# A third output tile in two PSUM banks, and a depthwise convolution's taps placed behind the softmax

## The chip, the cores and the metric

The kernel runs on one core of a Trainium2 chip. The metric is the device time of one execution in microseconds (us); the median of three executions before the change is 3747.22 us (3746.66 to 3749.31). Engines are named as in the profile: PE is TensorE (PEld its weight loads), DVE is VectorE, ACT is ScalarE, POOL is GpSimd, SP issues most of the transfers. All data are fp32. A difference of less than 0.2% is taken as no difference.

## The reference

The input x has 8 images of 384 channels and 64 x 64 pixels. Two layers follow each other, each added to its own input:

```python
x = x + attention(gn(x))     # layer norm, qkv, windowed attention, projection
x = x + ffn(gn(x))           # 1x1 convolution, 8x8 transform, depthwise 3x3, gate, 1x1 convolution
```

`gn` is a group normalisation over an image. The attention works in windows of 8 x 8 pixels, with 4 heads of 48 channels in plain windows (branch 0) and 4 in windows shifted by 4 pixels (branch 1): softmax(q k^T + position bias + mask) v, then a projection. The second layer is

```python
t = conv1x1(x, w_in); t = irfft2(rfft2(t in 8x8 patches) * filter)
t = depthwise3x3(t, w_dw)              # 9 taps for each channel
g = gelu(t[:192]) * t[192:]
y = conv1x1(g, w_out)                  # 192 -> 384 channels
```

The last line is the one whose third output tile the change splits.

## The kernel before

An image is cut into 8 strips of 8 rows (512 pixels). 384 channels are three tiles of 128 partitions. Every step of a strip is a small Python function, and a plan gives each step a place in time, counted in units: a unit is one attention branch of one strip, so an image has 16 units. The steps of all images are sorted by place and issued in that order (L803 to L819). The second layer of an image runs in the units of the next ones: while the attention of image b + 1 passes through its units, the strips of image b go through `normal_x1`, `mix`, `transform`, `back`, `conv`, `gate` and `finish`, one strip for two units. `finish` of a strip stands at place 0.10 of an even unit, 8 units or more after the start of the next image. So every even unit from unit 8 of image 1 on has one finish (images and units are counted from 0): 52 of them beside attention, and 12 in the tail after the last image's attention.

On PE the program's order is kept (`matmul`, L61). On DVE, ACT and POOL a scheduler of the framework orders instructions inside their dependencies, and moves some forward where it expects the engine to be idle; `behind` (L289) gives it an extra ordering on one engine. `conv` (L658) does one tap of the depthwise convolution for one channel tile m, the first tap on ACT (L667) and eight on DVE (L673). Taps 1 to 5 have places soon after the strip's `back` (for m = 0 in the same even unit, 0.68 to 0.92; for m = 2 and 1 in the odd one), taps 6 to 8 in the next even unit. Tap 6 is ordered behind the softmax's subtraction (`zs["soft"]`, L463).

The order of an even unit on PE is: `back` (pz), `apply` of the unit before (pA), `scores` (pS), `finish` (pw), the first `qk_tile` (pq), `put` of the unit before (po), then `mix` (pt) and `qk_tile` in turn, `turn` (pT), `v_tile` (pvv) and the layer norm's sums (ln). On DVE `normalise` (L503, L504) reads pA, `weights` (L456 to L463) reads pS and makes the softmax's exponents, L706 in `finish` adds pw to the residual, L535 to L537 move po.

[...] Tag "gemm" (`psum`) has four buffers of one bank: pq, pvv, ln, pt, pf, pz, pr and pw. Tag "att" (`psum2`) has two buffers of two banks: pS, pT, pA, po, and for the last image pc. A pool's buffers go round in order of allocation, and an allocation waits until the readers of the buffer's last tile are done.

`finish` makes its three output tiles from g0 (128 channels) and g1 (64 channels, held twice, in partitions 0 to 63 and 64 to 127). The g1 part is done by matmuls of 64 rows and 64 columns, a quarter of the array each, half naming the columns and r the rows:

```python
for m, half, r in ((0, 0, 0), (1, 1, 1), (0, 1, 0), (1, 0, 1), (2, 0, 0), (2, 1, 1)):
```

Then g0's part of each tile is accumulated by a full matmul, and DVE adds the tile to the residual.

A last piece is a plan of empty instructions. PE's runs of small tiles (pA, pS and their neighbours) need many instructions in little time. `FETCHES` has for every step how many instructions PE fetches (four for a matmul, two for a transpose), `WAITS` estimates those that only wait, and at the places of `small_tiles` the loop at L805 adds so many NoOps to the dense steps before (`qk_tile`, `project`) that the run begins at a given place (`RUN_AT`) of 256; if 100 or more would be needed, none are added.

Of the kernel before, what the change touches and what calls it, by code (L numbers as in the profile page):

```python
# [9 lines left out]
ALU = mybir.AluOpType  # L10
AX = mybir.AxisListType

P = 128
KC = 3
# [3 lines left out]
ST = WS * SW  # L18
# [10 lines left out]
N_CONST = C_SWAP + 128  # L29
WAITS = 5.325, -22  # L30
FETCHES = {"qk_tile": 12, "v_tile": 24, "project": 12, "scores": 128, "apply": 128, "turn": 16, "put": 16,
           "ln_sums": 64, "mix": 12, "transform": 32, "back": 192, "finish": 36, "input_mean": 4,
           "input_std": 4, "second_mean": 4, "second_std": 4, "filter_weights": 4, "out_bias": 36,
           "qk_weights": 48, "v_weights": 60}
RUN_AT = 208, 138
# [3 lines left out]
def block_kernel(ctx: ExitStack, tc: tile.TileContext, out, x, consts, fsel, wqk, wv, bqk, bv,  # L39
                 wp, bp, lng, lnb, rpb1, rpb2, w_in, w_dw, w_out, filt):  # L40
    nc = tc.nc
    B = x.shape[0]
# [7 lines left out]
    def psum(name):  # L50
        return ps.tile([P, ST], F32, tag="gemm", name=name)

    def psum2(name):

        return ps.tile([P, 2, ST], F32, tag="att", bufs=2, name=name)
# [5 lines left out]
    def matmul(*args, **kw):  # L61
        tc.keep_in_program_order(nc.tensor.matmul(*args, **kw))  # L62
        fetched["count"] += 4

        n = min(fetched["empty"], fetched["share"])
        for _ in range(n):
            tc.keep_in_program_order(nc.tensor.nop(hint="empty"))
        fetched["empty"] -= n
        fetched["count"] += n
# [5 lines left out]
    def strip(tag, bufs, name):  # L75
        return sb.tile([P, KC, ST], F32, tag=tag, bufs=bufs, name=name)

    def row512(tag, bufs, name):
        return sb.tile([P, ST], F32, tag=tag, bufs=bufs, name=name)
# [4 lines left out]
    def rows_of(img, s):  # L84

        return img[:, s * WS:(s + 1) * WS, :].rearrange("(p k) h w -> p k (h w)", k=KC)

    first_x = []
    for s in range(NS):
        tag, bufs = ("x", 5) if s < 5 else (("xn", 1), ("ow", 1), ("y2", 1))[s - 5]  # L90
        t = strip(tag, bufs, f"x_first{s}")
# [28 lines left out]
    wo_sb = cp.tile([P, 2, C], F32, name="wo_sb")  # L120
# [44 lines left out]
    for br, tab in ((0, rpb1), (1, rpb2)):  # L165
        raw = sb.tile([P, 2, 64], F32, tag="t2", bufs=3, name=f"rpb_raw{br}")
        raw_bias.append(raw)
        for h in range(4):
            half = slice(h % 2 * 64, h % 2 * 64 + 64)
# [110 lines left out]
    xs, ys, y2s, qks, vs, os_, ots, x1s, zs = ({} for _ in range(9))  # L280
# [8 lines left out]
    def behind(i, other, kind, reason):  # L289
        tc.add_manual_dep(i.ins, other.ins.name, mybir.DependencyInfo(kind, mybir.DependencyReason.DATA),  # L290
                          reason=reason)
# [366 lines left out]
    def conv(b, s, m, tap):  # L658

        z = zs[b, s, m]  # L660
        n = on_pe[s].get(m, 0) if b == B - 1 else 0
        if tap < max(n, 1):
            return
        if tap == max(n, 1):
            zz = row512("zz", 5, f"zz_{b}_{s}_{m}")
            if n == 0:
                nc.scalar.activation(zz.rearrange("p (r c) -> p r c", c=SW), z[:, 1:9, 1:SW + 1], AF.Copy,  # L667
                                     scale=dw_sb[:, m, 4:5])
                zs[b, s, "zz", m] = zz
            zs[b, s, "acc", m] = zz  # L670
        acc, old = zs[b, s, "acc", m], zs[b, s, "zz", m]
        dy, dx = TAPS[tap] // 3, TAPS[tap] % 3
        i = nc.vector.scalar_tensor_tensor(acc.rearrange("p (r c) -> p r c", c=SW),  # L673
                                           z[:, dy:dy + 8, dx:dx + SW], dw_sb[:, m, TAPS[tap]:TAPS[tap] + 1],
                                           old.rearrange("p (r c) -> p r c", c=SW), ALU.mult, ALU.add)

        if b < B - 1 and m and tap == 1:
            tc.keep_in_program_order(i)
        if b < B - 1 and tap == 6:
            behind(i, zs["soft"], mybir.DependencyClass.NoSync, "softmax first")  # L680
        zs[b, s, "zz", m] = acc

# [10 lines left out]
    def finish(b, s):  # L693


        g0, g1 = zs[b, s, "g"]
        t = xs[b, s, "finish"]
        pw = [psum(f"pw_{b}_{s}_{m}") for m in range(KC)]

        for m, half, r in ((0, 0, 0), (1, 1, 1), (0, 1, 0), (1, 0, 1), (2, 0, 0), (2, 1, 1)):  # L700
            rows, cols = slice(r * 64, (r + 1) * 64), slice(half * 64, (half + 1) * 64)
            matmul(pw[m][cols], wo_sb[rows, 1, m * P + half * 64:m * P + half * 64 + 64], g1[rows],
                   start=True, stop=False)
        for m in range(KC):
            matmul(pw[m], wo_sb[:, 0, m * P:(m + 1) * P], g0, start=False, stop=True)
            zs["added"] = nc.vector.tensor_tensor(t[:, m, :], pw[m], t[:, m, :], ALU.add)  # L706
        nc.sync.dma_start(out=rows_of(out[b], s), in_=t)


# [3 lines left out]
    for b in range(B):  # L713
# [62 lines left out]
        for s in range(NS):  # L776
            u = first + 2 + 2 * s
            at(u - 0.84, load, b, s, "mix")
            at(u + 0.02, normal_x1, b, s)
            for i in range(4):  # L780
                at(u + (0.28, 0.45, 0.60, 0.78)[i], mix, b, s, i)
            for j in range(2):
                at(u + (0.995, 1.02)[j], transform, b, s, j)
            if b < B - 1:
                at(u + 1.985, small_tiles, u + 2)
            at(u + 1.99, back, b, s)

            for n, m in enumerate((0, 2, 1)):
                for tap in range(1, 6):
                    at(u + (2.62, 3.15, 3.5)[n] + 0.06 * tap, conv, b, s, m, tap)  # L790
                for tap in range(6, 9):
                    at(u + 4.2 + 0.25 * (n * 3 + tap - 6) / 9, conv, b, s, m, tap)
            if b == B - 1:
                at(u + 2.3, conv_taps, b, s)
            at(u + 5.16, load, b, s, "finish")
            at(u + 4.5, gate, b, s)
            at(u + 6.10, finish, b, s)
# [7 lines left out]
    for i, (piece, args) in enumerate(order):  # L805
# [5 lines left out]
        elif piece is small_tiles:  # L811
            n = (RUN_AT[args[0] % 2] - count - round(WAITS[0] * args[0] + WAITS[1])) % 256
# [115 lines left out]
```

## Time and profile before

| what | before |
|---|---|
| median of three executions | 3747.22 us |
| profiled execution, its time | 3747.89 us |
| its span | 3745.9 us |
| PE busy | 3638.7 us, 97% of the span |
| PE weight loads | 2315.4 us, 62% |
| DVE busy | 2838.6 us, 76% |
| ACT busy | 2378.3 us, 63% |
| POOL busy | 439.2 us, 12% |
| HBM traffic | 99 GB/s over the span |
| granted TensorE clock | 0.996 |

The span is what the trace covers; the execution's own time has 2 us more around it. The busy time of PE is modelled at the ends of matmuls, so that 97% says that PE always has something in hand, not that every part of its array works. In the groups, the line L62 is the helper that records all matmuls, so matmuls are told apart by their tiles: pw is finish's.

### The profile page before, as it was taken

Reading aid. Unit: us, or ns where it says so; the run is one execution under the profiler, and the core shown is the slowest. Engines: PE = TensorE matmul, PEld = TensorE weight load, DVE = VectorE, ACT = ScalarE, POOL = GpSimd, SP = SyncE. Lnnn points to the kernel's source line nnn. Section 1 sums busy time; section 2 is a strip of 40 time slices with the busy share of each in tenths; the row PEclk is TensorE's granted clock in tenths of the full one; section 3 lists DMA queues with packets and bytes.
Section 4 is the critical chain, followed back from the end, with each engine's and each line's share of the span. In section 5 each row is a group of like instructions: output and inputs, shape, how many; then the busy total and the mean of one; then the engine's idle time right before and its main releaser. Section 6 shows DMA issues by size and latency. Waiting matters only on the chain.

```text
span 3745.9 us, 92754 instructions
## 1 busy us (share of the span) xinstructions
PE 3638.7 (97%) x38144; PEld 2315.4 (62%) x38144; DVE 2838.6 (76%) x4601; ACT 2378.3 (63%) x3946; POOL 439.2 (12%) x776
## 2 busy tenths in 40 slices
PE   4999999999999999999999999999999999999898
PEld 3666666666666666666666666666666666666554
DVE  4554578777887687777887778877788777777898
ACT  1766676666676576665766766666676666676442
POOL 5111011111101011101101011111111111110000
PEclk9999999999999999999999999999999999999999
DMA  4222222323322233323332322323233222222422
GB/s 121 86 83 74 91 100 100 107 90 108 118 103 83 88 133 108 116 80 116 109 113 84 117 95 100 133 80 109 99 113 109 99 88 83 100 80 82 151 102 76
DMA packets 144506, 377.32 MB, mean 101 GB/s; under 512 B 12308, under 2 KB 12900, under 8 KB 144100
## 3 DMA queue, kind: packets, MB, share of 16 engines
q1 hardware_dynamic: 139952, 370.60, 28.3%
q8 instruction: 318, 5.21, 0.6%
q0 software_dynamic: 2048, 0.15, 0.1%
q10 hardware_dynamic: 2100, 0.63, 0.1%
q14 instruction: 88, 0.72, 0.1%
HBM read 270.54 MB, written 100.79 MB: 99 GB/s over the span
## 4 chain that ended last, share of the span: by engine, by line
PE 84%; DVE 6%; ACT 4%; DMA 3%; issue 2%; POOL 0%; SPq 0%; ACTq 0%; DVEq 0%; POOLq 0%
PE pq L62 23%; PE pr L62 13%; PE pt L62 12%; PE pvv L62 12%; PE pw L62 6%; PE pS L62 3%; PE pA L62 3%; PE pz L62 3%; DVE zz L673 3%; PE pT L72 3%; PE po L72 2%; PE pf L62 2%; PE ln L62 2%; PE pc L62 1%; DMA rpb_raw<-in_rpb_dram 1%
## 5 line engine op out<-in xcount | busy, mean ns | idle before, releaser
L673 DVE SCALAR_TENSOR_TENSOR zz<-z,dw_sb,zz 128x512 f32<-128x512 f32 x1490 | 1105.9, 760 | 195.4 <-ACT zz L667 172.7
L62 PE MATMUL pq<-y,wqk_sb 128*128 128x512 f32 x2160 | 990.2, 596 | 0.0
L62 PEld LDWEIGHTS pq<-y,wqk_sb 128*128 128x128 f32 x2160 | 402.7, 190 | 456.2 <-issue 424.2
L62 PE MATMUL pt<-wi_sb,xn 128*128 128x384 f32 x1536 | 535.2, 487 | 8.1 <-DVE x_finish L706 8.1
L62 PE MATMUL pr<-oT,wp_sb 128*128 128x512 f32 x1152 | 523.1, 592 | 1.0 <-DVE oT L537 1.0
L62 PE MATMUL pvv<-wv_sb,y 128*128 128x192 f32 x2880 | 496.5, 326 | 2.5 <-ACT kcd L394 2.5
L62 PEld LDWEIGHTS pvv<-wv_sb,y 128*128 128x128 f32 x2880 | 471.6, 190 | 40.1 <-issue 21.3
L394 ACT ACTIVATE qab<-pq,bq_sb,cst 96x512 f32<-96x512 f32 (+1 forms) x256 | 198.0, 773 | 402.9 <-PE pq L62 386.0
L62 PEld LDWEIGHTS pt<-wi_sb,xn 128*128 128x128 f32 x1536 | 286.0, 190 | 213.9 <-issue 49.0
L394 ACT ACTIVATE kcd<-pq,vec 32x512 f32<-32x512 f32 x512 | 348.9, 681 | 9.0
L62 PEld LDWEIGHTS pr<-oT,wp_sb 128*128 128x128 f32 x1152 | 211.1, 190 | 224.4 <-issue 209.7
L376 POOL COPY y<-y 128x384 f32<-128x384 f32 x112 | 100.2, 894 | 1583.1 <-PE pvv L62 1089.3
L349 DVE TENSOR_TENSOR lr<-m 128x128 f32<-128x128 f32 x64 | 19.7, 308 | 301.9 <-ACT m L347 301.8
L335 POOL TENSOR_TENSOR sq<-sq 128x512 f32<-128x512 f32 x128 | 167.8, 1311 | 637.2 <-ACT sq L333 632.2
L667 ACT ACTIVATE zz<-z,dw_sb 128x512 f32<-128x512 f32 x183 | 133.8, 733 | 166.1 <-PE pw L62 160.5
L394 ACT ACTIVATE qcd<-pq,bq_sb,cst 96x512 f32<-96x512 f32 (+1 forms) x256 | 197.3, 771 | 43.8 <-PE pq L62 40.4
L546 DVE SCALAR_TENSOR_TENSOR x_add<-pr,vec,x_add 128x512 f32<-128x512 f32 x192 | 143.4, 747 | 103.3 <-PE pr L62 101.5
L584 ACT COPY t<-pt 128x384 f32<-128x384 f32 x256 | 125.0, 488 | 141.6 <-PE pt L62 138.7
L428 ACT COPY v<-pvv 128x384 f32<-128x384 f32 x256 | 121.8, 481 | 129.7 <-PE pvv L62 129.3
L62 PE MATMUL pw<-zz,wo_sb 128*128 128x512 f32 x384 | 181.9, 610 | 0.0
L394 ACT ACTIVATE kab<-pq,vec 96x512 f32<-96x512 f32 (+1 forms) x256 | 174.4, 681 | 9.1 <-PE pq L62 7.4
L469 ACT ACTIVATE e<-e 128x1024 f32<-128x1024 f32 x128 | 135.3, 1057 | 68.2 <-DVE e L463 66.8
(139 smaller groups left out, 5272.6 us busy)
## 6 DMA issues: line engine op xcount, KB each, us to landing
x_add<-in_x_dram SPq DMA_DIRECT2D x64, 768.0 KB
x1d<-x_add SPq DMA_DIRECT2D x64, 768.0 KB
x_mix<-x1d SPq DMA_DIRECT2D x64, 768.0 KB
x_finish<-x1d SPq DMA_DIRECT2D x64, 768.0 KB
out_dram<-x_finish SPq DMA_DIRECT2D x64, 768.0 KB
x_norm<-in_x_dram SPq DMA_DIRECT2D x61, 768.0 KB
x_stats<-in_x_dram SPq DMA_DIRECT2D x56, 768.0 KB
rs<-line SPq DMA_DIRECT2D x62, 256.0 KB
```

The source lines that it names most:

```text
L62: tc.keep_in_program_order(nc.tensor.matmul(*args, **kw))
L72: tc.keep_in_program_order(nc.tensor.transpose(*args, **kw))
L335: nc.gpsimd.tensor_tensor(sq[:, 0, :], sq[:, 0, :], sq[:, k, :], ALU.add)
L349: nc.vector.tensor_tensor(rc, m[:, 0:P], m[:, 0:P], ALU.mult)
L376: nc.gpsimd.tensor_copy(dst[:, :, :, :, 0:4], src[:, :, :, :, 4:8])
L394: return nc.scalar.activation(dst[to:to + n], pq[of:of + n], AF.Identity, bias=bias[of:of + n], scale=scale)
L428: nc.scalar.copy(v[:, 2 * g:2 * g + 2, :, 0:HD], pvv[:, 0:384].rearrange("p (g h d) -> p g h d", g=2, h=4))
L469: nc.scalar.activation(e, e, AF.Exp)
L546: nc.vector.scalar_tensor_tensor(t[:, m, :], pr, bp_sb[:, m:m + 1], t[:, m, :], ALU.add, ALU.add)
L584: nc.scalar.copy(t1, pt[:, 0:C])
L667: nc.scalar.activation(zz.rearrange("p (r c) -> p r c", c=SW), z[:, 1:9, 1:SW + 1], AF.Copy, scale=dw_sb[:, m, 4:5])
L673: i = nc.vector.scalar_tensor_tensor(acc.rearrange("p (r c) -> p r c", c=SW), z[:, dy:dy + 8, dx:dx + SW], dw_sb[:, m, TAPS[tap]:TAPS[tap] ...
```

## The change

`finish` keeps two tiles in the gemm pool and takes its third from attention's pool: the first 256 pixels of tile 2 go to one bank of that buffer, the last 256 to the other. The g1 part of tile 2 becomes four quarter matmuls of 256 columns instead of two of 512, the g0 part two full matmuls of 256 columns instead of one of 512. The three adds follow after all matmuls in program order; the third reads both banks in one instruction. The count of finish in `FETCHES` becomes 48. In `conv`, tap 1 of tile 0 is ordered behind the softmax as tap 6 already was; taps 2 to 5 of tile 0 follow it, since each adds to the result of the one before. Where this holds (all images but the last), it is the softmax of branch 0 of the even unit in which the taps are placed.

```diff
@@ -29,7 +29,7 @@
 FETCHES = {"qk_tile": 12, "v_tile": 24, "project": 12, "scores": 128, "apply": 128, "turn": 16, "put": 16,
-           "ln_sums": 64, "mix": 12, "transform": 32, "back": 192, "finish": 36, "input_mean": 4,
+           "ln_sums": 64, "mix": 12, "transform": 32, "back": 192, "finish": 48, "input_mean": 4,
@@ -676,7 +676,7 @@
         if b < B - 1 and m and tap == 1:
             tc.keep_in_program_order(i)
-        if b < B - 1 and tap == 6:
+        if b < B - 1 and (tap == 6 or m == 0 and tap == 1):
             behind(i, zs["soft"], mybir.DependencyClass.NoSync, "softmax first")
         zs[b, s, "zz", m] = acc
@@ -695,15 +695,23 @@
         g0, g1 = zs[b, s, "g"]
         t = xs[b, s, "finish"]
-        pw = [psum(f"pw_{b}_{s}_{m}") for m in range(KC)]
-
-        for m, half, r in ((0, 0, 0), (1, 1, 1), (0, 1, 0), (1, 0, 1), (2, 0, 0), (2, 1, 1)):
+
+        pw = [psum(f"pw_{b}_{s}_{m}") for m in range(2)]
+        pw2 = psum2(f"pw2_{b}_{s}")
+        full, lo, hi = slice(0, ST), slice(0, 256), slice(256, ST)
+        pw = [(pw[0], 0, full), (pw[1], 1, full), (pw2[:, 0, lo], 2, lo), (pw2[:, 1, lo], 2, hi)]
+
+        for i, half, r in ((0, 0, 0), (1, 1, 1), (0, 1, 0), (1, 0, 1), (2, 0, 0), (3, 1, 1), (2, 1, 0), (3, 0, 1)):
+            p, m, tok = pw[i]
             rows, cols = slice(r * 64, (r + 1) * 64), slice(half * 64, (half + 1) * 64)
-            matmul(pw[m][cols], wo_sb[rows, 1, m * P + half * 64:m * P + half * 64 + 64], g1[rows],
+            matmul(p[cols], wo_sb[rows, 1, m * P + half * 64:m * P + half * 64 + 64], g1[rows, tok],
                    start=True, stop=False)
-        for m in range(KC):
-            matmul(pw[m], wo_sb[:, 0, m * P:(m + 1) * P], g0, start=False, stop=True)
-            zs["added"] = nc.vector.tensor_tensor(t[:, m, :], pw[m], t[:, m, :], ALU.add)
+        for p, m, tok in pw:
+            matmul(p, wo_sb[:, 0, m * P:(m + 1) * P], g0[:, tok], start=False, stop=True)
+        for m in range(2):
+            nc.vector.tensor_tensor(t[:, m, :], pw[m][0], t[:, m, :], ALU.add)
+        by_half = t[:, 2, :].rearrange("p (o n) -> p o n", o=2)
+        zs["added"] = nc.vector.tensor_tensor(by_half, pw2[:, :, lo], by_half, ALU.add)
         nc.sync.dma_start(out=rows_of(out[b], s), in_=t)
```

## The prediction

> **What bounds the kernel now.** I read the page's busy times and its chain first:
>
> ```profile
> span 3745.9 us, 92754 instructions
> PE 3638.7 (97%) x38144; PEld 2315.4 (62%) x38144; DVE 2838.6 (76%) x4601; ACT 2378.3 (63%) x3946; POOL 439.2 (12%) x776
> ...
> PE 84%; DVE 6%; ACT 4%; DMA 3%; issue 2%; POOL 0%; SPq 0%; ACTq 0%; DVEq 0%; POOLq 0%
> ```
>
> PE is busy for 97% and carries 84% of the chain; the rest is mostly the first 60 us and the last 220. Next the groups, kept apart by shape, and PE's own waits:
>
> ```profile
> L673 DVE SCALAR_TENSOR_TENSOR zz<-z,dw_sb,zz 128x512 f32<-128x512 f32 x1490 | 1105.9, 760 | 195.4 <-ACT zz L667 172.7 <-ACT z L632 10.9
> ...
> L62 PE MATMUL pw<-zz,wo_sb 128*128 128x512 f32 x384 | 181.9, 610 | 0.0
> ...
> L62 PE MATMUL pw<-g,wo_sb 64*64 64x512 f32 x768 | 131.6, 611 | 5.1 <-DVE g L688 5.1
> ```
>
> ```profile
> PE pz L62 <- DVE t L601: 8.9, 15, 3.0
> PE pt L62 <- DVE x_finish L706: 8.1, 6, 1.4
> ...
> PE pvv L62 <- ACT kcd L394: 2.5, 6, 0.6
> ```
>
> In the middle of the run PE waits for almost nothing: what shortens PE's own work there shortens the kernel, one for one. The one regular wait is pt's for the residual add, 6 times 1.35 us. Then one `finish` in the timeline (unit 10 of image 4), rows of PE, its weight loads and DVE:
>
> ```profile
> 1995.68 1.54 DVE L673 SCALAR_TENSOR_TENSOR zz<-z,dw_sb,zz 128x512 f32<-128x512 f32 x2 [3.60 <-ACT zz L667]
> ...
> 1996.11 0.25 PEld L62 LDWEIGHTS pw<-g,wo_sb 64*64 64x64 f32 x8
> ...
> 1996.16 1.93 PE L62 MATMUL pw<-g,wo_sb 64*64 64x512 f32 x11
> 1996.65 0.14 PEld L62 LDWEIGHTS pw<-g,wo_sb 64*64 64x64 f32 x2 [0.29 <-issue]
> 1997.08 0.14 PEld L62 LDWEIGHTS pw<-g,wo_sb 64*64 64x64 f32 x2 [0.29 <-issue]
> 1997.13 0.25 DVE L503 RECIPROCAL rc<-pA 128x16 f32<-128x16 f32 x1
> 1997.30 0.70 DVE L673 SCALAR_TENSOR_TENSOR zz<-z,dw_sb,zz 128x512 f32<-128x512 f32 x1
> 1997.92 0.95 DVE L504 TENSOR_TENSOR o<-pA,rc 128x768 f32<-128x768 f32 x1
> ...
> 1998.03 2.84 PE L62 MATMUL pw<-zz,wo_sb 128*128 128x512 f32 x6
> ```
>
> Each fp32 matmul shows as two loads and two matmul instructions. The first four quarter matmuls (eight loads in a bunch) run four at a time: two rounds of 0.43 us. The third tile's two run as a pair, two more rounds of 0.43 (loads at 1996.65 and 1997.08), with half of the array idle. And two taps stand on DVE before L503, so pA is released only at 1998.87, 2.7 us after pw begins.
>
> [...] Here a 512-column fp32 instruction takes 429 ns and a 192-column one (pvv, 12 in 1.95 us) 163[...]: so my estimate for 256 columns is 216 ns. [...]
>
> **The change, part by part.**
>
> *Third tile, part of g1.* It removes two rounds of 429 ns and adds two of 216: minus 0.43 us. All four quarters at short length are shown by pf (16 instructions of 192 columns in 0.66 us, 0.165 per four). Loads of 64x64 take 0.03 us each in a bunch, under the running round.
>
> *Third tile, part of g0.* Two instructions of 429 become four of 216: plus 0.006. Weights of 128x128 keep up at 192 columns (pvv), so they do at 256. The last add still covers 512 elements, 0.68 us. Net, minus 0.42 us a finish.
>
> *Buffers.* Attention's two double banks rotate pA, pS, [pw2], po. So pw2 waits until normalise (L503, L504) has read pA, and po for the bias adds L456 instead of L504. Behind pw2 on PE stand the rest of finish, the pq of the unit and everything after it. Its first load is due 0.49 us after pw begins, its matmul at 0.92. pA ends 0.72 before pw; in the built order L503 now follows at once, since the taps come after L463. L503 + L504 take 1.25: L504 ends at about +0.57 and the matmul could start at about +0.68 (0.1 for the handover, an estimate from L706 to pt). Hidden, 0.24 us to spare. DVE is idle by then: in these units its last other work ends 2.6 us or more before pw. Without that cover the stall is as long as DVE is late. po comes over 2.5 us after pw ends, the L456 are done at about +2: nothing.
>
> *Finish takes two gemm buffers instead of three.* The ring of four moves on by one: pt's first tile now takes a pz buffer that ACT has read, and no longer pw's first.
>
> *Taps.* In the even units five taps (3.7 us of DVE) move behind the softmax. L463 ends at about +7.3 (pw end 4.1, last add 0.7, L460 1.2, L463 1.2) where it was +9.4 or later, so the work after it ends at most 1.6 us later. DVE's idle time before L349 in the units concerned is 2.9 us at least; less 0.4 for the shorter unit, 0.9 is left. The next late item would be the layer norm's row, not needed for a unit more. These taps issue no DMA; SP's order stays, POOL's border memsets and ACT's zz move by a few places in units with idle time there.
>
> *Instruction blocks.* The built PE program has 768 fetches more and 636 NoOps fewer. The runs of small tiles begin at places 204 to 211 of 256, where they began at 198 to 211. Before, odd units lie 0.15 us on average over their shortest 25.73 at either end of this: nothing, plus or minus 2 us in all.
>
> Now the places that differ: units 2 and 4 of images 2 to 7, and the tail. Rows of DVE and PE there, image 3:
>
> ```profile
> 1329.47 1.46 DVE L328 TENSOR_SCALAR y<-x_norm,gs_a 128x512 f32<-128x512 f32 x3 [0.57 <-DMA x_norm<-in_x_dram]
> 1330.85 0.25 DVE L503 RECIPROCAL rc<-pA 128x16 f32<-128x16 f32 x1
> 1331.14 0.96 DVE L504 TENSOR_TENSOR o<-pA,rc 128x768 f32<-128x768 f32 x1
> ```
>
> ```profile
> 1350.67 2.22 PE L62 MATMUL pvv<-wv_sb,y 128*128 128x192 f32 x12 [0.36 <-ACT kcd L394]
> ...
> 1390.20 2.20 PE L62 MATMUL pt<-wi_sb,xn 128*128 128x384 f32 x6 [1.35 <-DVE x_finish L706]
> ```
>
> *Unit 2.* pw begins at 1330.29, L504 ends at 1332.10 (+1.80) behind work that keeps its place, so pw2 stalls. In the six images L504 ends at +1.66, 1.80, 2.04, 1.89, 1.04, 0.62: over +0.75 (here the first two rounds are done at 0.86) that is 4.7 us. PE's pvv wait later in the unit (0.3 to 0.6, five times, 2.2) hangs on a chain that begins with L463, which comes about 3 us earlier: gone.
>
> *Unit 4.* L504 ends at +1.35 (last image 0.55). There pw's other buffers were late too (zz at +2.18); with the stall zz begins at about +1.97: minus 0.21 five times, 0.42 once. The pt wait of 1.35 goes: 8.1.
>
> *Tail, 12 finishes.* The first is bound by DVE (no idle from 3479 to 3516), the next two or three too (PE waits 2.97 and 1.24 for L601): nothing. Then six periods of 21.14 us in which PE is first and DVE only 0.2 us behind: 0.2 each, 1.2. The very last, 0.4.
>
> Sum: 40 ordinary finishes x 0.414 = 16.6; unit 2: 6 x 0.414 - 4.7 + 2.2 = 0.0; unit 4: 1.5 + 8.1 = 9.6; tail 1.6. Together 27.8 us. The profiled execution took 3747.9 (span 3745.9), so 3720.1; it is 0.7 over the median of 3747.2, so 3719.4.
>
> **Rivals.**
>
> *A, the waits at the image's start only change their owner.* pt or a later tile waits for something else, pvv's wait stays: 27.8 - 8.1 - 2.2 = 17.5, so 3730. For it: two engines are close together there. Against: the built pt waits for ACT alone, done 5 us earlier.
>
> *B, quarters don't run four at a time at 256 columns.* Four rounds of 216 take what two of 429 took: only 16.6 + 2.5 + 1.5 + 1.6 are lost, and about 5 is left: 3742. Against it, pf.
>
> *C, slower: pw2's wait decides.* If DVE reaches L503 late in the ordinary units, because the moved taps push the odd unit's work, PE stands at pw2. It breaks even when L504 ends at +1.22, DVE 0.65 us late. Late by 1.5 us, each of the 40 stalls 1.26: 50 us against 27.8, so 3770. For it: before, L504 did end at +2.7. Against: DVE's 2.6 idle us ahead, and 0.9 left before L349.
>
> *D, slower: the fetch plan, measured for the old count, misses.* A run that is caught loses up to 1.05 us (seen at 3451). With 0.35 us on 104 runs, 36: 3756. Against: the places are old ones.
>
> **How the numbers follow.** The sum 0.71, its own range 3714 to 3726 (L504's stalls and fetches, a few us each way; below 3714 if unit 2 doesn't stall and runs are caught less); A 0.14; B 0.06; C 0.05; D 0.04. I say 3719.5. From 3712 to 3735 at least 0.8 is held. 0.2% is 7.5 us, about what a measurement of this kernel tells from no change: B lies within it (with a part of D 0.07); the rest of C and D make 0.08 slower; the sum and A 0.85 faster.
>
> **What would show it.** pw<-g to pw<-zz 1.45 us apart instead of 1.87 in ordinary even units, which last 28.97 instead of 29.39; PE's wait for x_finish gone; a new wait pw2 <- DVE o L504 of 0.3 to 1.3 us in unit 2 only and 0.5 in unit 4; L503 within 0.1 us of pA's end. It would be wrong if that wait came in every even unit, if the pw<-g group stayed at 1.87, or if pT waited longer for e in odd units.

## The result and the profile after

The changed kernel takes 3715.66 us (median of 4 executions, 3713.22 to 3717.37), the kernel before, run beside it, 3746.94 us (4 executions, 3746.18 to 3749.31). The ratio is 0.9918, 95% interval 0.9906 to 0.993: faster by 31 us. Forecast were 3719.5 us, 3712 to 3735. The profiled execution took 3717.37 us against 3747.89 before, so 30.5 us are to be explained.

First the page of the changed kernel: its span, its busy times and its chain.

```profile
span 3715.4 us, 92922 instructions
PE 3609.1 (97%) x38528; PEld 2340.4 (63%) x38528; DVE 2844.0 (77%) x4601; ACT 2383.0 (64%) x3946; POOL 435.1 (12%) x776
...
PE 86%; DVE 6%; DMA 4%; ACT 2%; issue 1%; POOL 0%; SPq 0%; DVEq 0%; ACTq 0%; POOLq 0%
```

PE's busy time fell by 29.6 us and its span by 30.5. DVE does the same work as before. The time came out of what PE does and waits for, as it should in a kernel whose chain is PE's.

Next PE's waits (in us: the total, how often, the longest).

```profile
PE pz L62 <- DVE t L601: 10.8, 15, 3.2
PE pT L72 <- ACT e L469: 9.9, 8, 1.5
...
PE pw L62 <- DVE o L504: 6.1, 6, 1.3
```

The waits of pt for x_finish (8.1) and of pvv for kcd (2.5) are no longer in the list. A new one stands there: the third tile waits for `normalise`, 6 times in the whole run.

Then one `finish` in the timeline, unit 10 of image 4 again (start, duration, instruction, and in brackets the engine's idle time before it).

```profile
1983.59 0.26 DVE L503 RECIPROCAL rc<-pA 128x16 f32<-128x16 f32 x1 [3.94 <-PE pA L62]
...
1983.88 0.96 DVE L504 TENSOR_TENSOR o<-pA,rc 128x768 f32<-128x768 f32 x1
...
1984.18 0.25 PEld L62 LDWEIGHTS pw<-g,wo_sb 64*64 64x64 f32 x8
...
1984.24 1.51 PE L62 MATMUL pw<-g,wo_sb 64*64 64x512 f32 x15
...
1984.95 0.34 PEld L62 LDWEIGHTS pw<-g,wo_sb 64*64 64x64 f32 x8 [0.52 <-PE pS L62]
...
1985.68 2.85 PE L62 MATMUL pw<-zz,wo_sb 128*128 128x512 f32 x8
```

Before, the second bunch of loads was two pairs 0.43 us apart; now all eight come together, so the third tile's g1 part runs in four quarters. From the first quarter matmul (1984.23) to the first full one (1985.68) 1.45 us pass, where it was 1.87. L503 follows at the end of pA, after DVE has stood idle for 3.94 us, where two taps stood in front of it; L504 ends at 1984.84, before the second bunch of loads, and PE waits for nothing.

To see where the time went I divided both traces at the first pA of every unit and summed the lengths (an ordinary unit is an even one with a finish, other than units 2 and 4; most last 28.97 us after and 29.39 before):

| stretch | before, us | after, us | difference |
|---|---|---|---|
| 40 ordinary units with a finish | 1270.01 | 1252.66 | -17.35 |
| unit 2 of images 2 to 7 | 181.22 | 181.32 | +0.10 |
| unit 4 of images 2 to 7 | 188.20 | 177.70 | -10.51 |
| odd units of images 2 to 7 | 1157.15 | 1157.26 | +0.11 |
| images 0 and 1 without their finishes, start | 698.13 | 698.13 | 0.00 |
| tail | 251.22 | 248.30 | -2.92 |

### The profile page after: what moved, and what is told of

The parts are those of the page before. It is cut to its first block, busy times and chain, and to the rows that moved or that the text cites. A ratio compares the mean times of both kernels' runs of the same rounds, so it can differ in the third digit from the quotient of the medians.

```text
span 3715.4 us, 92922 instructions
## 1 busy us (share of the span) xinstructions
PE 3609.1 (97%) x38528; PEld 2340.4 (63%) x38528; DVE 2844.0 (77%) x4601; ACT 2383.0 (64%) x3946; POOL 435.1 (12%) x776
## 4 chain that ended last, share of the span: by engine, by line
PE 86%; DVE 6%; DMA 4%; ACT 2%; issue 1%; POOL 0%; SPq 0%; DVEq 0%; ACTq 0%; POOLq 0%
PE pq L62 24%; PE pr L62 13%; PE pvv L62 12%; PE pt L62 12%; PE pw L62 6%; DVE zz L673 3%; PE pS L62 3%; PE pA L62 3%; PE pT L72 3%; PE po L72 3%; PE pz L62 3%; PE pf L62 2%; PE ln L62 2%; DMA x_norm<-in_x_dram 1%; DMA rpb_raw<-in_rpb_dram 1%
## 5 line engine op out<-in xcount | busy, mean ns | idle before, releaser
L673 DVE SCALAR_TENSOR_TENSOR zz<-z,dw_sb,zz 128x512 f32<-128x512 f32 x1490 | 1081.8, 751 | 23.7 <-ACT z L632 11.2
L62 PE MATMUL pw<-zz,wo_sb 128*128 128x512 f32 (+1 forms) x512 | 182.4, 499 | 0.0
L72 PEld LDWEIGHTS pT<-cst,e 128*128 128x128 f32 x1024 | 119.1, 141 | 67.2 <-issue 39.8
```

Of the source, the lines that this page charges most:

```text
L72: tc.keep_in_program_order(nc.tensor.transpose(*args, **kw))
```

## The experiments

Each is a whole kernel and leaves out nothing of the computation. The first four were compared with the kernel before at 3746.38 us (median of 22 executions), the last two at 3746.18 us (15).

**The split alone.** The taps go back to where they were.

```diff
-        if b < B - 1 and (tap == 6 or m == 0 and tap == 1):
+        if b < B - 1 and tap == 6:
```

> The third tile split as in the change, the taps left where they were before it. Theory (the split pays only because the taps were moved away from in front of normalise): L504 ends where it ended before, 2.7 to 4.7 us after pw begins in 40 ordinary even units, so pw2 stands 1.9 to 3.9 us in each, 111 us in all; less the 28 us of the change, 3825 us (3800 to 3840), with a wait pw <- o L504 of about 110 us. Rival (DVE's taps were moved for another reason, pw2's buffer is free anyway): 3716 to 3722 us, no such wait.

Measured: 3887.93 us (4 executions, 3867.6 to 3895.56), ratio 1.0374 (1.0349 to 1.04). Slower, and more than expected. The waits of PE:

```profile
PE pw L62 <- DVE o L504: 105.5, 46, 3.7
...
PE pvv L62 <- ACT kcd L394: 6.2, 8, 1.2
```

In 46 of the 52 units with a finish beside attention (all but unit 4 of images 2 to 7) the third tile now waits for `normalise`. So the moved taps aren't a refinement beside the split: without them it loses. In a typical such unit L504 ends 2.71 us after pw's start and the tile's first matmul comes at +2.86; with the taps moved these are +0.61 and +0.86. So the tile comes 2.0 us late in such a unit, and 3 to 4 where DVE is later. There is no wait of pt for x_finish in the list, but pvv's wait for kcd has grown from 2.5 us before to 6.2: I come back to both.

The waits don't hold all of the loss: against the changed kernel the 40 ordinary units are 167.5 us longer, and the wait for L504 only grew from 6.1 to 105.5. The rest is in the clock. A table of stretches, columns: the length, PE's busy time and instructions, the same for loads, DVE, ACT and POOL, the granted clock, the transfers:

```profile
2009.00:2012.00 3.00, 1.67 (x62) 0.79 (x54) 1.22 (x2) 2.77 (x10) 2.13 (x3) 1.00 0.00 0
2012.00:2015.00 3.00, 0.73 (x8) 0.33 (x8) 3.00 (x6) 0.00 (x0) 0.00 (x0) 0.76 0.00 0
2015.00:2018.00 3.00, 3.00 (x7) 1.17 (x4) 2.20 (x4) 0.00 (x0) 0.00 (x0) 0.50 0.03 8
2018.00:2021.00 3.00, 3.00 (x8) 1.89 (x7) 1.12 (x3) 0.29 (x1) 0.00 (x0) 0.60 0.00 0
```

PE stood idle from 2010.7 to 2014.3 for L504, and works at half clock until after 2018. Its matmuls say the same: in this finish the full 512-column instructions start 853 ns apart instead of 429, the 256-column ones 427 instead of 216. Over the run 25 of the 46 finishes whose third tile comes over 1 us late have such doubled distances, 58 us in all (the time from the first quarter of the third tile to the next step's first matmul, less its length elsewhere). The third tile comes 116.5 us late in these 46 finishes, counted from its place at +0.86, against 7.7 in six of the changed kernel: 109 and 58 together are 167 of the 170 us between the two profiled executions. The stall that was expected, 111 us, is nearly right; the half clock is what the 3825 lacked.

**The taps alone.** The kernel before with the new line of `conv`, the third tile as it was.

```diff
-        if b < B - 1 and tap == 6:
+        if b < B - 1 and (tap == 6 or m == 0 and tap == 1):
```

> Only the taps moved, finish as before. Theory of the prediction (in unit 4 the pt wait went because the ring of gemm buffers moved on): the pt wait of 6 x 1.35 us stays, only pvv's wait of 2.2 us goes: 3745 us. Rival (moving the taps alone ends it, since L706 no longer stands behind five taps and comes about 4 us earlier): both waits go, 10 us less: 3737 us. Either way the ordinary even units stay at 29.39 us.

Measured: 3729.04 us (5 executions, 3728.23 to 3730.49), ratio 0.9958 (0.9944 to 0.9971): 17 us faster. Both figures given beforehand are missed. The ordinary units keep their 29.39 us; unit 2 gives 4.3 us and unit 4 gives 9.7 (six of each). The other 3.5 lie in no single place (odd units 1.7, tail, start and ordinary units some 0.6 each). PE's longest waits of this kernel:

```profile
PE pT L72 <- ACT e L469: 9.5, 8, 1.5
PE pz L62 <- ACT v L428: 6.7, 13, 1.0
PE pw L62 <- DVE g L688: 5.1, 1, 5.1
```

The waits of pt and pvv are gone from this list too, with three gemm buffers still in use. In unit 4 of image 3 the three adds and pt, first before, then with the taps alone:

```profile
1387.23 2.31 DVE L673 SCALAR_TENSOR_TENSOR zz<-z,dw_sb,zz 128x512 f32<-128x512 f32 x3
...
1389.46 1.88 DVE L706 TENSOR_TENSOR x_finish<-pw,x_finish 128x512 f32<-128x512 f32 x3
...
1390.20 2.20 PE L62 MATMUL pt<-wi_sb,xn 128*128 128x384 f32 x6 [1.35 <-DVE x_finish L706]
```

```profile
1381.25 0.69 DVE L706 TENSOR_TENSOR x_finish<-pw,x_finish 128x512 f32<-128x512 f32 x1 [0.17 <-PE pw L62]
...
1384.50 2.10 PE L62 MATMUL pt<-wi_sb,xn 128*128 128x384 f32 x6
```

Before, three taps stand right ahead of the adds, and pt stands behind the first of these. With the taps behind the softmax it is DVE that waits for the matmuls (0.17 us before the last add, the one shown), and this add is done 2.6 us before pt begins. So pt has two ways out of its wait: earlier adds (this run), or another buffer (the split alone, where the adds were still late and the wait was gone all the same). But only the first of them saves the time. In the split alone unit 4 is 2.2 us shorter for all six, where the wait of pt alone had been 8.1: PE now waits in pvv for kcd there, 0.9 to 1.2 us each time, a wait that stood in unit 2 before. The softmax is as late as before in that unit (L463 ends at +13.3), and with the taps behind it this second wait goes too. So what rival A feared, a wait that only changes its owner, is what the split does by itself.

**The third tile in one bank.** The taps are moved and the tile is taken from attention's pool, but whole and in one of its banks, with two quarter matmuls of 512 columns as before.

```diff
-        pw = [psum(f"pw_{b}_{s}_{m}") for m in range(KC)]
+        pw = [psum(f"pw_{b}_{s}_{m}") for m in range(2)] + [psum2(f"pw2_{b}_{s}")[:, 0]]
```

> The taps moved and the third tile in attention's buffer, but whole, in one bank, with the old two quarter matmuls of 512 columns and one full matmul of 512. Theory (0.41 us of each finish comes from four quarters at a time): ordinary even units stay at 29.39 us; pt's and pvv's waits go (10 us), pw2's stalls of unit 2 come (6): 3743 us (3740 to 3746). Rival (the gain is that of buffers and taps, not of the array): 3716 to 3722 us.

Measured: 3738.09 us (18 executions, 3734.34 to 3740.45), ratio 0.9978 (0.9971 to 0.9985), between the two figures given beforehand: the theory took the taps for 10 us, and they are worth 17. The ordinary units are back at 29.39 us, as in the kernel before. Unit 10 of image 4 and the wait of unit 2:

```profile
1990.14 1.93 PE L62 MATMUL pw<-g,wo_sb 64*64 64x512 f32 x11
...
1992.01 0.70 PE L62 MATMUL pw<-zz,wo_sb 128*128 128x512 f32 x1
```

```profile
PE pw L62 <- DVE o L504: 3.9, 6, 0.9
```

From the first quarter matmul to the first full one 1.87 us pass again. By units the changed kernel gains 17.1 us on this one in its 40 ordinary units (0.43 each) and 2.6 in the tail. So the gain of the split is that the third tile's four quarters run together, and not the other pool or the moved taps. Four quarters in a single bank were not tried, so that the third tile needs two banks for them was not shown. Moving the tile to attention's pool costs by itself: unit 2 is 4.6 us longer than with the taps alone, for a wait of 3.9 for L504.

**Normalise first.** The changed kernel, with the group normalisation (L328) of strips 3 and 4 ordered behind L504. These are the strips whose L328 stood ahead of L503 in units 2 and 4.

```diff
-            nc.vector.tensor_scalar(by_window(y[:, k, :]), image_order(t[:, k, :]), gs[:, 0:1], gs[:, 1:2],
-                                    ALU.subtract, ALU.mult)
+            i = nc.vector.tensor_scalar(by_window(y[:, k, :]), image_order(t[:, k, :]), gs[:, 0:1], gs[:, 1:2],
+                                        ALU.subtract, ALU.mult)
+            if b and s in (3, 4):
+                behind(i, zs["normalised"], mybir.DependencyClass.NoSync, "attention's output first")
...
-        nc.vector.tensor_tensor(
+        zs["normalised"] = nc.vector.tensor_tensor(
```

> The changed kernel, with the group normalisation (L328) of strips 3 and 4 ordered behind the normalise (L504) of the attention branch before it on DVE, in every image but the first. Theory (pw2's stall of 6.1 us in unit 2 is L503 standing behind L328, which waits for its transfer): the wait pw <- o L504 falls from 6.1 to below 1 us and the time by 6 to 7 us, to about 3709 us. Rival (the layer norm's chain that begins with L328 becomes late, and its waits come back as pT or ln): 3714 to 3722 us.

Measured: 3705.77 us (4 executions, 3702.13 to 3706.69), ratio 0.9894 (0.9881 to 0.9908). It is 10 us under the changed kernel's median, more than the 6 to 7 expected; its profiled execution took 3704.87. Unit 2 of image 3 in the timeline, first of the changed kernel, then of this one (where lines are 2 higher from L330 on):

```profile
1324.47 1.46 DVE L328 TENSOR_SCALAR y<-x_norm,gs_a 128x512 f32<-128x512 f32 x3 [0.94 <-DMA x_norm<-in_x_dram]
...
1325.85 0.25 DVE L503 RECIPROCAL rc<-pA 128x16 f32<-128x16 f32 x1
1326.13 0.96 DVE L504 TENSOR_TENSOR o<-pA,rc 128x768 f32<-128x768 f32 x1
...
1327.23 0.66 PE L62 MATMUL pw<-g,wo_sb 64*64 64x256 f32 x8 [1.20 <-DVE o L504]
```

```profile
1319.36 0.26 DVE L505 RECIPROCAL rc<-pA 128x16 f32<-128x16 f32 x1 [0.77 <-PE pA L62]
1319.65 0.96 DVE L506 TENSOR_TENSOR o<-pA,rc 128x768 f32<-128x768 f32 x1
...
1320.02 1.51 PE L62 MATMUL pw<-g,wo_sb 64*64 64x512 f32 x14
```

In the changed kernel DVE waits for a strip from HBM until 1324.47 and then normalises it for 1.46 us, while pA, ready at 1324.2, stands behind it in DVE's order. Now `normalise` waits for pA alone; the third tile follows without a gap. Unit 2 falls from 30.2 us on average to 28.97, the length of an ordinary unit: 7.5 us for the six, for a wait of 6.1; unit 4 gives 1.7 more. This version beats both kernels.

**Without the empty instructions.** The loop that adds NoOps never adds any.

```diff
-            if n < 100:
+            if n < 0:
```

> The changed kernel without its 3902 empty PE instructions; nothing else differs, the computation is whole. It measures what is at stake in rival D, the fetch plan: the runs of small tiles now begin anywhere in a block of 256 instructions. If a run that is caught loses up to the 1.05 us seen once before the change and about one in three of 104 runs is caught, the time is some 35 us longer: 3750 (3735 to 3770), and units that were 28.97 scatter. Rival: crossings are hidden[...], and the empty instructions cost or bring nothing: 3713 to 3719, and then rival D never had anything to decide.

Measured: 3746.55 us (12 executions, 3741.56 to 3747.59), ratio to the kernel before 0.9999 (0.999 to 1.0007): without the plan the whole gain of the change would be gone. PE's waits, first of the changed kernel, then of this one ("issue" is time in which the engine waits for nothing that the profile shows):

```profile
PE pS L62 <- issue: 2.7, 5, 0.9
...
PE pA L62 <- issue: 0.8, 2, 0.5
```

```profile
PE pS L62 <- issue: 24.0, 32, 2.8
...
PE pA L62 <- issue: 2.9, 7, 0.6
```

Most of the loss lies in the runs of small tiles (in unit 10 of image 4 of the changed kernel 30 matmuls of pS take 0.69 us), 0.75 us each in 32 of pS; with those of pA and three of pw these waits grew by 25 us of the 31 lost, and the rest is not accounted for. Ordinary even units (unit 0 and the last image apart) scatter from 28.97 to 30.49 us; with the plan most of them are 28.97. That these waits recur with a period of 256 instructions can be counted: along PE's instructions in the trace (loads, matmuls, semaphore waits), 40 of the 42 waits with no other cause stand at place 193 or 194 of 256. The counting begins at the trace's first instruction, so this place says nothing of where a block of the plan begins. In dense work no such wait shows (none of the 42 is one of pq, pr, pt or pvv); in runs of small tiles it does. So rival D was about a real stake of 30 us, and with the plan it did not happen: in the changed kernel 5 such waits are left at that place, 2.7 us in all. Whether the new count of 48 was needed for it was not tried.

**The scaling later too.** The version with normalise first, and in unit 3 the layer norm's scaling behind the softmax's subtraction.

```diff
-        nc.vector.tensor_tensor(y, y, rs.unsqueeze(1).to_broadcast([P, KC, ST]), ALU.mult)
+        i = nc.vector.tensor_tensor(y, y, rs.unsqueeze(1).to_broadcast([P, KC, ST]), ALU.mult)
+        if b and s == 3:
+            behind(i, zs["soft"], mybir.DependencyClass.NoSync, "softmax first")
```

> The kernel of the run with normalise first, and besides the layer norm's scaling of strip 3 (L363 of the changed kernel) ordered behind the softmax's subtraction, in images 1 to 7. In the trace of that run the scaling (1.76 us) stands on DVE between the maximum and the subtraction of unit 3, and PE waits 0.97 to 1.26 us for the exponents there, 7 times, 7.7 us in all; moved, it lets the subtraction start 1.7 us earlier. Theory (what PE waits for in the middle of the run is lost one for one): 3705.8 - 7.7 = 3698 (3695 to 3701), and one wait of pT for e is left, the last of the run. Rival: the scaled strip is late for POOL's copies and for the next unit's projections, so that the wait only changes its owner: 3703 to 3712, with a new wait of pq for the copies of L376.

Measured: 3697.55 us (4 executions, 3697.13 to 3698.4), ratio 0.987 (0.9854 to 0.9887). The number is met, its reason only in part. Unit 3 of the six images is 10.8 us shorter (1.8 each, more than the wait; where the rest comes from is open), and unit 4 is 6.0 us longer, for the wait that the version before had got rid of:

```profile
PE pw L62 <- DVE o L508: 4.8, 5, 1.6
```

In unit 4 of image 3 the row of DVE shows whom it waits behind:

```profile
1362.87 1.88 DVE L237 BATCH_NORM_STATS2 st<-x_stats 128x6 f32<-128x512 f32 x3 [0.45 <-DMA x_stats<-in_x_dram]
...
1364.78 0.26 DVE L507 RECIPROCAL rc<-pA 128x16 f32<-128x16 f32 x1
...
1366.18 0.66 PE L62 MATMUL pw<-g,wo_sb 64*64 64x256 f32 x8 [0.69 <-DVE o L508]
```

PE reaches unit 4 earlier, and another strip from HBM, that of the statistics, is now what `normalise` stands behind. Moving these statistics wasn't tried. It is still the fastest of the kernels here.

## Why the prediction was right

**Four quarters instead of two, minus 0.42 us a finish.** Right: 1.445 us from pw's first matmul to the first full one where 1.45 was said, and even units of 28.97 us where 28.97 was said. The price of 216 ns for 256 columns, the author's estimate (a straight line through the measured 429 ns for 512 columns and 163 for 192 gives it too), is what the full matmuls of the two halves show: 216 ns from start to start. Rival B is out by this, and by the one-bank run. The 40 ordinary units gave 17.35 us; 16.6 were said, for the sum takes 0.414 us each where its own parts make 0.42.

**The third tile's wait is hidden.** Right in the ordinary units. L503 starts 0.08 us after pA's end (within 0.1 was said), L504 ends at +0.605 (+0.57 was said), the third tile's first matmul is at +0.86 (its place behind the first rounds was said to be +0.92). The split alone shows that it is hidden by the taps' move and nothing else. Rival C's mechanism is real, then; only its condition was missing. Its price in the prediction, 1.26 us for each stall, was too low: most stalls are 2 us or more, and the half clock wasn't in it.

**Taps behind the softmax.** L463 ends at +7.4 where +7.3 was said, and what came later on DVE held up PE by little: the odd units of images 2 to 7 are the same within 0.11 us in 1157. One sign that was named for being wrong, a longer wait of pT for e in odd units, did come, though small: 9.9 us where it was 9.0.

**Unit 2, nothing gained.** Said 0.0, measured +0.10, by luck: two errors cancel. The stall was said to be 4.7 us; counted the same way (L504's end over +0.75) it is 7.5, and the profile has 6.1 of idle time. The step took the ends of L504 from the trace of before, "behind work that keeps its place", but that work waits for a transfer, which comes later against a PE that is ahead ([0.94 <-DMA x_norm] where it was 0.57). L504 ended at +2.23 to +1.68 after pw's start, where +2.04 to +0.62 were taken. On the other side the moved taps gave more than the wait of pvv, 2.2: the taps alone gave 4.3 in unit 2.

**Unit 4, minus 9.6.** Measured 10.5, with the wrong cause. The step "Finish takes two gemm buffers instead of three. The ring of four moves on by one" was credited with the 8.1 us of pt's wait. The split alone ends this wait by the new buffer, but gains only 2.2 us in unit 4, 1.5 of which were said for the split itself, since pvv's wait takes its place; the taps alone give 9.7. So nearly all of unit 4's gain comes from the taps and needs no split, and that the number was met is luck. The prediction followed one release of pt and did not ask what PE would wait for next. The stall itself was small: zz begins at +2.09 where +1.97 was said.

**Tail, 1.6.** Measured 2.9. The steady period between finishes fell from 21.14 us to 20.85, 0.29 where 0.2 was taken; there are five such periods and not six, so 1.5 in all where 1.2 was said. The stretch after them gave 0.4, as said. The others, taken as nothing, moved too: the last before the steady ones from 22.18 to 20.70 us, the rest by 0.3 at most, up or down. That one fell is luck in part: before, its first 2.2 us run at half clock (granted 0.50 until 3583.08 us), which costs 1.1; after, the half clock ends as it begins.

**Rival A** (the waits only change owner) is out in this kernel: neither wait came back under another name. In the split alone and in the last experiment just that happened.

**A regular wait that was not seen.** The prediction calls pt's wait the one regular wait in the middle of the run. The list of before has another:

```profile
PE pT L72 <- ACT e L469: 9.0, 8, 1.4
```

Seven of these eight stand in unit 3 of images 1 to 7. The forecast didn't suffer, since the change leaves them (9.9 us after); the last experiment gains from them.

**Where 30.5 comes from.** Not 27.8: 0.7 more in the ordinary units, 0.9 in unit 4, 1.3 in the tail. Split by edits it reads otherwise than the prediction had it: the taps alone are worth 17.3 us in the medians, and the split adds 13.4 on top of them (in the profiled executions 13.0: some 17 in the ordinary units, 2 in the tail and 1 in unit 4, less 4.4 in unit 2 and 2.4 elsewhere).

## What to carry to other kernels

When a tile takes a buffer from another ring, ask whose release it now waits for, and bring that reader forward in the same change: the same split is worth minus 13 us or plus 142 us, by what stands ahead of two small DVE instructions. When a wait disappears, test each edit alone before one of them is credited with it, and measure the stretch it stood in: a wait that is gone from the list may stand there under another name. Work that waits for a transfer should not stand in an engine's order ahead of work that PE waits for (moving it gave 10 us here); where PE got ahead of the transfers, that wait grew (0.57 to 0.94 us in unit 2 of image 3).

## What was not expected of the hardware

In the split alone PE went on at half clock after 25 of the 46 stalls for the third tile. Of 18 finishes whose third tile came 2.9 us late or more 16 did; of 21 where it came 1.9 to 2.2 us late 9 did; of the 13 with 0.9 to 1.5 us, in that run and in the changed kernel, none.

In the trace of that run the granted clock changes only in steps of 3.413 us, on one grid from the start to the end of the run. Here are two stalls of the split alone on this grid, one of 1.78 us (from 2072.2) and one of 2.70 (from 2244.4), with the columns of the table above:

```profile
2071.58:2075.00 3.42, 1.64 (x17) 0.53 (x10) 3.42 (x7) 0.05 (x1) 0.00 (x0) 1.00 0.00 0
2075.00:2078.41 3.41, 3.41 (x6) 1.65 (x5) 2.39 (x5) 0.00 (x0) 0.00 (x0) 0.50 0.02 5
...
2242.25:2245.67 3.42, 2.16 (x98) 1.28 (x86) 2.07 (x4) 2.35 (x9) 1.72 (x3) 1.00 0.02 5
2245.67:2249.08 3.41, 1.97 (x11) 0.91 (x12) 3.41 (x6) 0.00 (x0) 0.15 (x1) 1.00 0.00 0
2249.08:2252.49 3.41, 3.41 (x11) 1.90 (x10) 3.38 (x6) 0.72 (x1) 0.00 (x0) 1.00 0.02 5
```

The shorter stall lies inside one step: PE is busy for 1.64 us of it, and the next step runs at half clock. The longer one is shared by two steps, each with about 2 us of work, and the clock stays. Between 100 us and the tail 25 steps at full clock were followed by one at half clock, one for each of the 25 finishes, and in all of them PE was busy for 1.64 us or less. Of the other 973 only 8 are as low (1.63 to 1.64). So work in up to 48% of a step did not keep the clock up in 25 of 33 cases, and what decides among these was not shown. Before and in the changed kernel no step of this part has under 1.9 us of work, and none is followed by half clock.

The four executions of the split alone spread from 3867.6 to 3895.56 us, where the others lie within 7. The shortest has the highest granted clock, 0.986 against 0.978 and 0.979. Why the clock differs from one execution to the next was not tested.
